# Graph attention and neighbour quantiles on one core: finer pieces of the first search, larger pieces of the quantile sort, the last attention tile in three turns, another order of the units

## The chip, the cores and the metric

One Trainium2 chip, one of its cores. The time is the device time of one execution in microseconds; below, "the profiled execution" is one more execution, taken with the hardware profiler.

## The reference, cut to what matters

There are 4,096 nodes with 128 features and a 0/1 matrix `adj` of 4096 x 4096 with about 32 neighbours in a row. Two layers follow each other.

```python
# layer 0: graph attention, 8 heads
Wh = einsum('nd,hde->hne', x, W)
f1 = einsum('hnd,hd->hn', Wh, a1);  f2 = einsum('hnd,hd->hn', Wh, a2)
e = leaky_relu(f1[:, :, None] + f2[:, None, :], 0.2)
att = softmax(where(adj > 0, e, -9e15), axis=-1)
cat = heads side by side of elu(att @ Wh)
x1 = layernorm(x + elu(cat @ W1 + b1)) * gamma + beta
# layer 1: quantiles over a thinned neighbour list
keep = neighbours whose rank is not a multiple of ceil(number / 2)
agg = mean over q in (0.25, 0.5, 0.75) of the value at place ceil(q * n_keep) - 1
      in each feature's sorted kept neighbours of x1
out = (0.5 * agg + 0.5 * x1) @ Wl.T + bl + x1
```

## The kernel before, in words

Nodes are handled in 32 tiles of 128. The order of instructions on VectorE, TensorE, ScalarE and GpSimd is the order in which the program writes them (`manual_schedule(engines=ORDERED)`); the DMAs of SyncE are placed by the framework. Generators that `yield` are woven into one another by hand, and each yield ends a "piece".

**The first search** (`neighbours`, L624, over the 6 tiles of the first block) turns rows of `adj` into lists of neighbours. Halves of a tile's rows are loaded from ScalarE's DMA queue into three buffers (L635), ScalarE takes their sign (L642), TensorE makes keys from it, 512 columns at a time (two products a piece, L681 and L684), and VectorE finds the largest eight of each 128 (L648) and merges them (L653, L655). There are 8 pieces to a tile. In these pieces `tile_gat_quantile_kernel` (L323 to L326) calls once per piece the generator `node_rows` (L542), which prepares what the gathers read later: it loads W, a1, a2, Wl and x on ScalarE's queue, forms `wa` = W a on VectorE (L565, L568), transposes x tile by tile on TensorE (L585), copies the result on ScalarE (L587), multiplies it by `wa` (L579), copies that (L574), clips it, and stores each node's row with its f2 in `xt_d` (L592). It works on four tiles at a time: in one piece the four transposes and a copy, in the next four products.

**The attention** runs over blocks of 6, 10 and 16 tiles. `fetch_rows` (L909) gathers up to 64 neighbour rows per partition, one indirect DMA of GpSimd a slot, 16 slots to a buffer `G`. `attend` (L935) weighs a tile: add f1 and f2 (L949), leaky relu (L955), exp (L956), per-node sums on TensorE (L964), reciprocal (L974, L975), spreading it back (L980), the product (L991), the block matrix `wide` (L999), and one product a slot into `y` (L1012). It then says "summed", and its tail (from L1024: W, elu, W1, layer norm) is woven into the next tile's head by `step` (L371). The search of the next block is woven in as well. The very last tile has nobody behind it. Its x1 is scattered to `x1_d` (L369), and then the quantiles can start.

**The quantiles**: after all 32 tiles, the tiles are sorted again in 21 units: [0], [1], the pairs [2,3] to [22,23], and [24] to [31]. For a unit, GpSimd gathers its neighbours' x1 slot by slot into one of two buffers `vals` and its own rows into `xs` (L507 to L517). The queue of GpSimd holds, in this order: the gathers of unit i+1, the writes of unit i-1 (L519, which wait for its result on ScalarE), the gathers of unit i+2, and so on; those of a unit wait until the unit two before has read its `vals`. `quantile_out` (L1168) runs a selection network on VectorE: minima and maxima of two runs of slots (L1225), between two work buffers and into `goal`. After a certain time on VectorE, estimated by `then` (L1191), the loop issues `turn_of_gpsimd` (L1194), a copy of one element from PSUM, and starts to count anew. It cuts longer runs:

```python
if then(c * m) > TURN_MAX:            # too long for this turn
    room = int((TURN_AIM - then(0)) / (size * TT_EACH))
...
if ran > TURN_MIN:
    turn_of_gpsimd()
```

Then TensorE takes the weighed sum of the goals (L1244), adds half of x1 (L1251), ScalarE copies it (L1255), TensorE multiplies by Wl (L1258 to L1262), ScalarE copies (L1270), and GpSimd scatters the result to the output.

Of the kernel before, what the change touches and what calls it, by code (L numbers as in the profile page):

```python
# [22 lines left out]
H = 8  # L23
# [219 lines left out]
def kernel(  # L243
# [127 lines left out]
    def step(fetch=None, soon=(), pieces=None, quota=0, first=False, among=()):  # L371
        if first:
            keep_x1(fetch)
        if fetch:
            weigh.append(fetch_rows(tc, attp, fetch, xt_d, list(among)))
        if not first:
            keep_x1(fetch)
        done = 0
        each = quota / STEPS
        head = None  # L380
        if len(weigh) > 1 or (weigh and not fetch):
            head = attend(tc, attp, pp, weigh.pop(0), consts)
# [159 lines left out]
def node_rows(tc, sp, pp, rec, x, W, W_sb, a1, a2, Wl, wa, WlT, ident, bad, xt_d):  # L542
# [28 lines left out]
    xT = f_ps = None  # L571
    for t in range(0, NT + 8, 4):
        if f_ps is not None:
            nc.scalar.copy(F[:, t - 8 : t - 4, :], f_ps)  # L574
            f_ps = None
        if xT is not None:
            f_ps = pp.tile([P, 4, 2 * H], F32, name="f_ps")
            for u in range(4):
                nc.tensor.matmul(f_ps[:, u, :], lhsT=xT[:, ts(u, P)], rhs=wa, start=True, stop=True)  # L579
            xT = None  # L580
        yield
        if t < NT:
            xt_ps = pp.tile([P, 4 * P], F32, name="xt_ps")
            for u in range(4):
                nc.tensor.transpose(xt_ps[:, ts(u, P)], rec[:, t + u, R_X : R_X + D], ident)  # L585
            xT = sp.tile([P, 4 * P], F32, name="xT", bufs=2)
            nc.scalar.copy(xT, xt_ps)  # L587
        yield
# [343 lines left out]
    return R, mine, out  # L932


def attend(tc, ap, pp, fetched, consts):  # L935


    nc = tc.nc
    R, mine, parts = fetched
    own, ownT = consts["own"], consts["ownT"]  # L940
    slots = sum(w - g0 for w, g0, _, _ in parts)


    z = ap.tile([P, L, H], F32, name="z", bufs=2)
    layer = []
    a = 0
    for w, g0, runs, f1v in parts:
        for G, col, g, m in runs:
            nc.vector.tensor_tensor(  # L949
                z[:, a + g : a + g + m, :], G[:, col : col + m, D:], f1v[:, g : g + m, :], ALU.add  # L950
            )
        layer.append(a)
        a += w - g0
    zs = z[:, 0:slots, :].rearrange("p s h -> p (s h)")
    nc.vector.scalar_tensor_tensor(zs, zs, ALPHA, zs, ALU.mult, ALU.max)  # L955
    nc.scalar.activation(zs, zs, AF.Exp)  # L956
    yield

    small = consts["small"]
    den = small[:, 0 : 32 * H]  # L960
    for i, (w, g0, runs, f1v) in enumerate(parts):
        k = P // w
        for r in range(k // 4):
            nc.tensor.matmul(  # L964
                den[0:4, :].rearrange("p (g r h) -> p r g h", r=k // 4, h=H)[:, r, g0:],
                lhsT=own[w][:, ts(r, 4)],
                rhs=z[:, layer[i] : layer[i] + w - g0, :],
                start=(i == 0 and r == 0),
                stop=(i == len(parts) - 1),
                skip_group_check=True,  # L970
            )
    yield
    rden = ap.tile([4, 32 * H], F32, name="rden", bufs=1)
    nc.vector.tensor_scalar(rden, den[0:4, :], TINY, None, ALU.max)  # L974
    nc.vector.reciprocal(rden, rden)  # L975
    rz = pp.tile([P, L * H], F32, name="rz")
    for i, (w, g0, runs, f1v) in enumerate(parts):
        k = P // w
        for r in range(k // 4):
            nc.tensor.matmul(  # L980
                rz[:, layer[i] * H : (layer[i] + w - g0) * H],
                lhsT=ownT[w][:, r, :],
                rhs=rden.rearrange("p (g r h) -> p r g h", r=k // 4, h=H)[:, r, g0:],
                start=(i == 0 and r == 0),
                stop=(r == k // 4 - 1),
                skip_group_check=True,
            )
            if r % 8 == 7:
                yield
    yield  # L990
    nc.vector.tensor_tensor(zs, zs, rz[:, 0 : slots * H], ALU.mult)  # L991

    y = pp.tile([P, 2, 512], F32, name="y")
    yf = y.rearrange("p a b -> p (a b)")
    for i, (w, g0, runs, f1v) in enumerate(parts):
        k, n = P // w, w - g0
        pf = ap.tile([P, H * P], F32, name="wide")
        spread = [P, n, k, H]
        nc.vector.tensor_tensor(  # L999
            pf[:, 0 : n * k * H].rearrange("p (g k h) -> p g k h", g=n, k=k),  # L1000
            z[:, layer[i] : layer[i] + n, :].unsqueeze(2).to_broadcast(spread),
            own[w].unsqueeze(1).unsqueeze(3).to_broadcast(spread),
            ALU.mult,
        )
        yield
        c = k * H
        for G, col, a, m in reversed(runs):

            for j in reversed(range(a, a + m)):
                g = g0 + j  # L1010

                nc.tensor.matmul(  # L1012
                    yf[:, ts(g, c)],
                    lhsT=G[:, col + j - a, 0:D],
                    rhs=pf[:, ts(j, c)],
                    start=(i == 0 and g % (w // 2) == w // 2 - 1),
                    stop=(i == len(parts) - 1),
                    skip_group_check=True,
                )
                if g % 4 == 0:  # L1020
# [4 lines left out]
    nc.scalar.copy(  # L1025
        yT.rearrange("p h (u g) -> p g u h", u=4), yf.rearrange("p (g u h) -> p g u h", u=4, h=H)
    )
# [470 lines left out]
```

## Time and profile before

| | us |
|---|---|
| three runs | 3614.76, 3615.5, 3617.49 |
| median | 3615.5 |
| the profiled execution, its own time | 3611.84 |
| its span, first to last instruction | 3610.1 |
| VectorE busy | 2742.8 (76%), 7,591 instructions |
| GpSimd busy | 2344.3 (65%), 2,341 instructions |
| TensorE busy, its weight loads | 1258.1 (35%) and 951.4 (26%) |
| ScalarE busy | 399.5 (11%) |
| first gather of the attention / of the quantiles | 150.8 / 1828.3 |
| first and last tensor_tensor of the quantiles | 1857.3 / 3596.6 |

In the profile a row of a group gives the line, the engine, the operation, what is written from what, shapes, the count, busy time and mean, then how long the engine was idle before these instructions and who released it. A row of the timeline gives start, duration, engine, line, operation. DVE is VectorE, PE is TensorE and PEld its weight loads, ACT ScalarE, POOL GpSimd, SP SyncE. An fp32 product appears as two TensorE instructions.

### The profile page before, as it was taken

The numbers are of one execution on the slowest core, as the hardware profiler recorded it, in microseconds if no ns is written. First come the engines' busy times: TensorE is split into PE (matmuls) and PEld (weight loads), VectorE is DVE, ScalarE is ACT, GpSimd is POOL, SyncE is SP. The second block draws the span as 40 slices with busy tenths as digits, with TensorE's granted clock in tenths as the row PEclk, the third lists the DMA queues.
The fourth block names the chain that finished last, engine by engine and source line by source line (L and its number), as shares of the span: only waits on it lengthen the run. The fifth ranks groups of instructions, "written<-read, shape, count | busy, mean of one in ns | idle before, by whom it ended". The sixth has DMA issues, their size and how long they took to land. (4 is left out here: it accounts for less than half of the span.)

```text
span 3610.1 us, 22900 instructions
## 1 busy us (share of the span) xinstructions
PE 1258.1 (35%) x5323; PEld 951.4 (26%) x5323; DVE 2742.8 (76%) x7591; ACT 399.5 (11%) x555; POOL 2344.3 (65%) x2341
## 2 busy tenths in 40 slices
PE   6377667878456454456610000000000000001101
PEld 3044545445455454355510000000000000000101
DVE  7787548877345122157448999999999999999998
ACT  3122122322111011111110000000000000000000
POOL 1375767757777777777557776777555766667530
PEclk9965557566556555555555555555555555555555
DMA  6443244432222222222111111111111111111100
GB/s 212 132 147 90 67 149 139 142 123 70 59 63 55 55 55 54 66 58 55 43 38 48 48 47 41 46 47 46 39 34 37 47 44 40 43 45 47 38 20 3
DMA packets 109137, 237.46 MB, mean 66 GB/s; under 512 B 46720, under 2 KB 63104, under 8 KB 100800
## 3 DMA queue, kind: packets, MB, share of 16 engines
q0 software_dynamic: 74368, 156.34, 15.5%
q10 hardware_dynamic: 14848, 70.85, 5.7%
q1 hardware_dynamic: 19776, 8.73, 1.1%
q8 instruction: 44, 0.72, 0.1%
q14 instruction: 101, 0.83, 0.1%
HBM read 224.60 MB, written 11.15 MB: 65 GB/s over the span
## 5 line engine op out<-in xcount | busy, mean ns | idle before, releaser
L219 POOL DMA_INDIRECT G<-xt_d,idx x1124 | 1096.6, 976 | 416.3 <-issue 324.0
L219 POOL DMA_INDIRECT vals<-x_d,idx x1024 | 1052.3, 1028 | 333.9 <-issue 298.0
L1225 DVE TENSOR_TENSOR work<-work 128x512 f32<-128x512 f32 (+6 forms) x1405 | 959.4, 710 | 0.4
L1244 PE MATMUL st_ps<-dg,goal 128*128 128x128 f32 x286 | 71.8, 429 | 1644.7 <-DVE goal L1225 1574.6
L1225 DVE TENSOR_TENSOR work<-work,work 128x512 f32<-128x512 f32 (+5 forms) x958 | 604.9, 655 | 0.7
L1244 PEld LDWEIGHTS st_ps<-dg,goal 128*128 128x128 f32 x286 | 63.8, 324 | 1651.0 <-issue 1650.2
L1012 PE MATMUL y<-wide,G 128*128 128x32 f32 (+3 forms) x2248 | 482.7, 392 | 26.9 <-DVE wide L999 26.9
L1012 PEld LDWEIGHTS y<-wide,G 128*128 128x128 f32 x2248 | 461.2, 309 | 62.3 <-DVE wide L999 30.0
L648 DVE MAX8 first<-key 128x8 f32<-128x128 f32 x1024 | 225.2, 281 | 119.0 <-PE key L684 118.5
L949 DVE TENSOR_TENSOR z<-G,f1x 128x128 f32<-128x128 f32 (+5 forms) x92 | 29.0, 328 | 307.9 <-DMA G<-xt_d,idx 302.7
L228 POOL DMA_INDIRECT out_dram<-o,own_i x32 | 51.0, 1593 | 295.3 <-ACT o L1270 276.1
L681 PE MATMUL key<-sgn,markb 128*128 128x512 bf16 x256 | 149.3, 583 | 145.3 <-DVE first L648 98.2
L1196 DVE COPY junk<-still 128x1 f32<-128x1 f32 x1295 | 191.2, 148 | 0.0
L1225 DVE TENSOR_TENSOR work<-vals 128x1024 f32<-128x1024 f32 (+8 forms) x140 | 138.8, 1007 | 46.2 <-DMA vals<-x_d,idx 45.9
L642 ACT ACTIVATE sgn<-adj_t 128x2048 bf16<-128x2048 int32 x64 | 122.1, 1907 | 355.4 <-PE key L681 304.8
L1043 PE MATMUL small<-W_sb,late 128*128 128x128 f32 x512 | 126.0, 430 | 88.4 <-DVE late L1040 88.4
L1243 ACT ACTIVATE dg<-ident,wt 128x128 f32<-128x128 f32 x143 | 47.5, 393 | 955.9 <-PE st_ps L1244 955.6
L964 PE MATMUL small<-z,own 128*4 128x32 f32 (+6 forms) x438 | 49.6, 280 | 284.8 <-ACT z L956 284.8
L684 PE MATMUL key<-parts,oneb 64*128 64x512 bf16 x256 | 147.2, 575 | 0.2 <-POOL parts L237 0.2
L1043 PEld LDWEIGHTS small<-W_sb,late 128*128 128x128 f32 x512 | 111.7, 324 | 102.7 <-DVE late L1040 99.0
L980 PE MATMUL rz<-rden,ownT 4*128 4x32 f32 (+6 forms) x438 | 97.8, 386 | 78.0 <-DVE rden L975 63.0
L1031 PE MATMUL hT<-late,W_sb 128*128 128x128 f32 x512 | 110.9, 385 | 35.4 <-ACT late L1025 35.4
(184 smaller groups left out, 1763.3 us busy)
## 6 DMA issues: line engine op xcount, KB each, us to landing
adj_t<-in_adj_dram ACTq DMA_DIRECT2D x64, 1024.0 KB
G<-xt_d,idx POOLq DMA_INDIRECT x1124
vals<-x_d,idx POOLq DMA_INDIRECT x1024
R<-rec_d SPq DMA_DIRECT2D x128, 26.2 KB
xt_d<-rec SPq DMA_DIRECT2D x4, 544.0 KB
rec<-in_x_dram ACTq DMA_DIRECT2D x4, 512.0 KB
narrow<-rec_d SPq DMA_DIRECT2D x68, 5.2 KB
a_b<-in_L_gnn_a_dram ACTq DMA_DIRECT2D x2, 512.0 KB
```

The source lines that it names most:

```text
L219: nc.gpsimd.indirect_dma_start(out=dst, out_offset=None, in_=rows, in_offset=bass.IndirectOffsetOnAxis(ap=idx, axis=0),)
L642: nc.scalar.activation(sgn, adj_t, AF.Sign, accum_out=cnt[:, i : i + 1])
L648: nc.vector.max(first[:, ts(c0 // CW + c, 8)], key[:, ts(c, CW)])
L681: nc.tensor.matmul(key, lhsT=markb, rhs=sgn[:, ts(b, 512)], start=True, stop=False)
L684: nc.tensor.matmul(key, lhsT=oneb[0:64, :], rhs=parts[1][:, ts(r - 1, 512)] if r else parts[0], start=False, stop=True)
L980: nc.tensor.matmul(rz[:, layer[i] * H : (layer[i] + w - g0) * H], lhsT=ownT[w][:, r, :], rhs=rden.rearrange("p (g r h) -> p r g h", r=k // ...
L1012: nc.tensor.matmul(yf[:, ts(g, c)], lhsT=G[:, col + j - a, 0:D], rhs=pf[:, ts(j, c)], start=(i == 0 and g % (w // 2) == w // 2 - 1), stop= ...
L1031: nc.tensor.matmul(hT[:, ts(h, P)], lhsT=consts["W_sb"][:, h, :], rhs=yT[:, h, :], start=True, stop=True)
L1043: nc.tensor.matmul(o, lhsT=hv[:, h, :], rhs=consts["W1_sb"][:, h, :], start=(h == 0), stop=(h == H - 1))
L1196: nc.vector.tensor_copy(junk, late["still"])
L1225: nc.vector.tensor_tensor(slots_of(dst, (j, c, s, m), size), slots_of(a, (i, c, s, m), size), slots_of(b, (i + d, c, s, m), size), op,)
L1244: nc.tensor.matmul(st_ps[:, u, :], lhsT=goal[:, (j * k + u) * D : (j * k + u + 1) * D], rhs=dg, start=(j == 0), stop=False,)
```

## The change

Four parts in one edit.

```diff
-TURN_MIN, TURN_AIM, TURN_MAX = 1.25, 1.45, 1.7
+TURN_MIN, TURN_AIM, TURN_MAX = 1.1, 1.9, 2.4
```

The quantile loop cuts fewer runs of slots. By its own counting, with the constants before, it issues 2,649 tensor_tensors and 1,295 copies; with those after, 2,250 and 1,118, on the same elements.

```diff
-    order = UNITS[:1] + UNITS[2 + len(pairs) :] + pairs[::-1] + UNITS[1:2]
+    order = UNITS[:2] + UNITS[2 + len(pairs) :] + pairs[::-1]
```

Unit [1] is sorted second and not last; the pair [2,3] is now the last.

```diff
@@ node_rows
     load = nc.scalar.dma_start
+    for _ in range(4):
+        yield
     load(W_sb, W.rearrange("h d e -> d h e"))
-    yield
+    for _ in range(2):
+        yield
...
     for i in range(4):
-        for _ in range(3):
+        for _ in range(2):
             yield
...
+    LAG = 3
+    turned, f_ps = [], None
+    for t in range(NT + LAG):
+        if t < NT:
+            xt_ps = pp.tile([P, 4 * P], F32, name="xt_ps")[:, 0:P]
+            nc.tensor.transpose(xt_ps, rec[:, t, R_X : R_X + D], ident)
+            xT = sp.tile([P, P], F32, name="xT", bufs=LAG + 2)
+            nc.scalar.copy(xT, xt_ps)
+            turned.append(xT)
+        u = t - LAG
+        if u >= 0:
+            if u % 4 == 0:
+                f_ps = pp.tile([P, 4, 2 * H], F32, name="f_ps")
+            nc.tensor.matmul(f_ps[:, u % 4, :], lhsT=turned.pop(0), rhs=wa, start=True, stop=True)
+        yield
+        if u > 0 and u % 4 == 3:
+            nc.scalar.copy(F[:, u - 3 : u + 1, :], f_ps)
```

In the first search, one transpose with its copy and one product go into each piece; the product belongs to the tile three pieces back. W is loaded four pieces later, a1, a2 and Wl five. These rows now take 55 pieces where they took 39, of the search's 62.

```diff
@@ attend
+    turns = [(parts, 0)]
+    if last and [v[0:2] for v in parts] == [(32, 0)]:
+        w, g0, runs, f1v = parts[0]
+        turns = []
+        for m, (a, b) in enumerate(((0, 16), (16, 24), (24, 32))):
+            G, col, g, _ = runs[a // 16]
+            turns.append(([(w, a, [[G, col + a - g, 0, b - a]], f1v[:, a:b, :])], a))
...
+    for turn, (parts, a0) in enumerate(turns):
...
```

The body of `attend`, from the addition to the products into `y`, stands in this loop. For all tiles but the very last it runs once and issues what it issued before. For the last tile it runs over slots 0 to 15, 16 to 23 and 24 to 31 in turn, each with its own exp, sums, reciprocal, `wide` and products; `step` passes `last` when no fetch and no other tile follows.

More of the change, by code (lines that the diff above doesn't have):

```diff
@@ L381, in step @@
         if len(weigh) > 1 or (weigh and not fetch):
-            head = attend(tc, attp, pp, weigh.pop(0), consts)
+            last = not fetch and len(weigh) == 1
+            head = attend(tc, attp, pp, weigh.pop(0), consts, last)
         active = [v for v in (tail.pop() if tail else None, head) if v]
@@ L570, in node_rows @@
     F = sp.tile([P, NT, 2 * H], F32, name="F")
[L571 to L580, printed above, removed]
-        yield
[L582 to L588, printed above, removed]
+    LAG = 3
[12 more added lines that the diff above has]
+            nc.tensor.matmul(f_ps[:, u % 4, :], lhsT=turned.pop(0), rhs=wa, start=True, stop=True)
+        yield
+        if u > 0 and u % 4 == 3:
+            nc.scalar.copy(F[:, u - 3 : u + 1, :], f_ps)
     for dst, src in ((R_F1, F[:, :, 0:H]), (R_X + D, F[:, :, H:])):
@@ L932, in fetch_rows, with attend @@
     return R, mine, out
-def attend(tc, ap, pp, fetched, consts):
+def attend(tc, ap, pp, fetched, consts, last):
     nc = tc.nc
@@ L940, in attend @@
     own, ownT = consts["own"], consts["ownT"]
-    slots = sum(w - g0 for w, g0, _, _ in parts)
-    z = ap.tile([P, L, H], F32, name="z", bufs=2)
[L945 to L954, printed above, removed]
@@ L955, in attend @@
-    nc.vector.scalar_tensor_tensor(zs, zs, ALPHA, zs, ALU.mult, ALU.max)
-    nc.scalar.activation(zs, zs, AF.Exp)
-    yield
+    turns = [(parts, 0)]
[5 more added lines that the diff above has]
+            turns.append(([(w, a, [[G, col + a - g, 0, b - a]], f1v[:, a:b, :])], a))
+    z = ap.tile([P, L, H], F32, name="z", bufs=2)
@@ L959, in attend @@
     small = consts["small"]
     den = small[:, 0 : 32 * H]
[L961 to L971, printed above, removed]
@@ L972, in attend @@
-    yield
     rden = ap.tile([4, 32 * H], F32, name="rden", bufs=1)
-    nc.vector.tensor_scalar(rden, den[0:4, :], TINY, None, ALU.max)
-    nc.vector.reciprocal(rden, rden)
     rz = pp.tile([P, L * H], F32, name="rz")
[L977 to L989, printed above, removed]
@@ L990, in attend @@
-    yield
-    nc.vector.tensor_tensor(zs, zs, rz[:, 0 : slots * H], ALU.mult)
     y = pp.tile([P, 2, 512], F32, name="y")
     yf = y.rearrange("p a b -> p (a b)")
[L995 to L1004, printed above, removed]
+    opened = set()
@@ new lines, in attend @@
+    for turn, (parts, a0) in enumerate(turns):
+        whole = len(turns) == 1
+        layer = []
+        a = a0
+        for w, g0, runs, f1v in parts:
+            for G, col, g, m in runs:
+                nc.vector.tensor_tensor(
+                    z[:, a + g : a + g + m, :],
+                    G[:, col : col + m, D:],
+                    f1v[:, g : g + m, :],
+                    ALU.add,
+                )
+            layer.append(a)
+            a += runs[-1][2] + runs[-1][3]
+        zs = z[:, a0:a, :].rearrange("p s h -> p (s h)")
+        nc.vector.scalar_tensor_tensor(zs, zs, ALPHA, zs, ALU.mult, ALU.max)
+        nc.scalar.activation(zs, zs, AF.Exp)
@@ L1005, in attend @@
         yield
[L1006 to L1010, printed above, removed]
+        for i, (w, g0, runs, f1v) in enumerate(parts):
+            k = P // w
+            g1 = g0 + runs[-1][2] + runs[-1][3]
+            for r in range(k // 4):
                 nc.tensor.matmul(
[L1013 to L1016, printed above, removed]
+                    den[0:4, :].rearrange("p (g r h) -> p r g h", r=k // 4, h=H)[:, r, g0:g1],
+                    lhsT=own[w][:, ts(r, 4)],
+                    rhs=z[:, layer[i] : layer[i] + g1 - g0, :],
+                    start=(turn == 0 and i == 0 and r == 0),
@@ L1019, in attend @@
                 )
-                if g % 4 == 0:
-                    yield
+        yield
+        rd = rden if whole else rden[:, a0 * H : a * H]
+        nc.vector.tensor_scalar(
+            rd, den[0:4, :] if whole else den[0:4, a0 * H : a * H], TINY, None, ALU.max
+        )
+        nc.vector.reciprocal(rd, rd)
+        for i, (w, g0, runs, f1v) in enumerate(parts):
+            k = P // w
+            n = runs[-1][2] + runs[-1][3]
+            for r in range(k // 4):
+                nc.tensor.matmul(
+                    rz[:, layer[i] * H : (layer[i] + n) * H],
+                    lhsT=ownT[w][:, r, :],
+                    rhs=rden.rearrange("p (g r h) -> p r g h", r=k // 4, h=H)[:, r, g0 : g0 + n],
+                    start=(turn == 0 and i == 0 and r == 0),
+                    stop=(r == k // 4 - 1),
+                    skip_group_check=True,
+                )
+                if r % 8 == 7:
+                    yield
+        yield
+        nc.vector.tensor_tensor(zs, zs, rz[:, a0 * H : a * H], ALU.mult)
+        for i, (w, g0, runs, f1v) in enumerate(parts):
+            k, n = P // w, runs[-1][2] + runs[-1][3]
+            pf = ap.tile([P, H * P], F32, name="wide")
+            spread = [P, n, k, H]
+            nc.vector.tensor_tensor(
+                pf[:, 0 : n * k * H].rearrange("p (g k h) -> p g k h", g=n, k=k),
+                z[:, layer[i] : layer[i] + n, :].unsqueeze(2).to_broadcast(spread),
+                own[w].unsqueeze(1).unsqueeze(3).to_broadcast(spread),
+                ALU.mult,
+            )
+            yield
+            c = k * H
+            for G, col, a, m in reversed(runs):
+                for j in reversed(range(a, a + m)):
+                    g = g0 + j
+                    bank = g * c // 512
+                    nc.tensor.matmul(
+                        yf[:, ts(g, c)],
+                        lhsT=G[:, col + j - a, 0:D],
+                        rhs=pf[:, ts(j, c)],
+                        start=bank not in opened,
+                        stop=(i == len(parts) - 1),
+                        skip_group_check=True,
+                    )
+                    opened.add(bank)
+                    if g % 4 == 0:
+                        yield
     yield "summed"
```

## Prediction

> **What bounds the kernel now.** I read the busy shares and the 40 slices first. Each slice is 90 us.
>
> ```profile
> DVE  7787548877345122157448999999999999999998
> ...
> POOL 1375767757777777777557776777555766667530
> ```
>
> Three stages follow one another. The first search fills slices 1 and 2. After it GpSimd's gathers set the pace up to about slice 20. From slice 23 VectorE is at nine tenths or more, to the end. The busy times by stretch say the same: 896.7 of 1,630 us for VectorE between 150 and 1780 us, but 1,723.9 of 1,740 between 1857 and 3597. So a microsecond saved in the quantile stage on VectorE, or before the first gather, or between the last gather of the rows and the first one of the quantiles, comes off the end one for one.
>
> Next, VectorE's groups with the shapes kept apart, for what the quantile stage is made of (count, busy us, mean ns):
>
> ```profile
> L1225 DVE TENSOR_TENSOR work<-work 128x512 f32<-128x512 f32 x512 | 339.3, 682 | 0.1
> L1225 DVE TENSOR_TENSOR work<-work 128x1024 f32<-128x1024 f32 x273 | 334.2, 1229 | 0.0
> ...
> L1196 DVE COPY junk<-still 128x1 f32<-128x1 f32 x1295 | 191.2, 148 | 0.0
> ...
> L1225 DVE TENSOR_TENSOR work<-vals 128x512 f32<-128x512 f32 x21 | 13.8, 686 | 13.8 <-DMA vals<-x_d,idx 13.8
> ```
>
> These busy times overlap, so prices must be taken from start to start, in the timeline:
>
> ```profile
> 2311.64 0.68 DVE L1225 TENSOR_TENSOR work<-work 128x512 f32<-128x512 f32 x1
> 2312.17 0.97 POOL L219 DMA_INDIRECT vals<-x_d,idx  x1 [0.30 <-issue]
> 2312.23 0.42 DVE L1225 TENSOR_TENSOR work<-work,work 128x256 f32<-128x256 f32 x1
> 2312.57 0.42 DVE L1225 TENSOR_TENSOR work<-work 128x256 f32<-128x256 f32 x1
> 2312.90 0.15 DVE L1196 COPY junk<-still 128x1 f32<-128x1 f32 x1
> 2312.97 1.62 DVE L1225 TENSOR_TENSOR work<-work 128x256 f32<-128x256 f32 x3
> 2313.44 1.23 POOL L219 DMA_INDIRECT vals<-x_d,idx  x1 [0.30 <-issue]
> ```
>
> A 512 takes 0.59 to 0.61 us to the next start, a 256 0.34, a copy 0.07. Hence 1.054 ns an element, 0.067 us fixed for a tensor_tensor, 0.070 for a copy. Counting through the loop of quantile_out gives 1,382,784 elements, and the rows have 2,649 tensor_tensors: 1457.5 + 177.5 + 90.7 (1,295 copies) = 1725.7 us. Measured: 3596.6 - 1857.3 - 13.8 waiting = 1725.5. The prices hold.
>
> **Quantile pieces.** The same loop with 1.1/1.9/2.4 issues 2,250 tensor_tensors and 1,118 copies on the same elements. Saved: 399 x 0.067 = 26.7 and 177 x 0.070 = 12.4, together **39.1 us**, all on VectorE's path. The Trainium skill (Perfetto Trace Analysis, Optimizing Scalar/DVE Operations) puts a VectorE instruction's overhead at about 60 ns on SBUF and 125 ns on PSUM, and the copy reads PSUM; that would make 23.9 + 22.1 = 46.0. The copies here cost 0.070 from start to start, so I take 39.1. Bounds 33 (some overheads reappear as semaphore waits) to 46.
>
> What hides behind VectorE are the gathers: 0.94 us each and 0.30 of issue, a cycle of 1.25. A gather that is delayed ends 0.90 us after a boundary between two VectorE instructions: the one above starts at 2313.44, the next copy is at 2314.51, and it lasts 1.23 rather than 0.94. Of 1,038 gathers between 1860 and 3462 us, 930 go through beside a copy and 108 between two tensor_tensors. Here a rule speaks against the change: by the skill (SBUF — State Buffer, Who interferes with whom) a VectorE instruction with two SBUF inputs keeps out, for its whole length, a GpSimd instruction that reads SBUF. Pieces of up to 2048 elements (2.2 us) then hold a gather that much longer. I count with one gather a turn, and no gather cycle under 1.25 us. Turns now average 1.32 us, after the change 1.50.
>
> Is that enough? The pairs [18,19] down to [4,5] have 559 turns now and 434 after. While they are sorted, GpSimd must fetch the seven pairs [14,15] to [2,3] (402 gathers) and write 16 tiles: 418. So 16 turns are spare, some 25 us. Followed gather by gather (one per turn, vals free after its last read), the lead of a pair's last gather over its first tensor_tensor comes out within 7 us of the trace for today's kernel (140 against 139 at [18,19], 87 against 87 at [4,5]). After the change it falls from 115-123 us at [18,19] to 22 at [2,3], and VectorE never waits in the pairs. By the rule without spare turns it would wait; by this count, no cost.
>
> **Two short units first.** VectorE waits twice at the start: 22 gathers, then 13.8 us for [24] (the row above). With [1] second, its 22 gathers fit beside the sort of [0] (35 us). But [24] then needs 22 + 1 + 36 gathers from 1857, at some 1.33 each 79 us, plus 1.65 to land, against 67 us of sorting: the wait only moves, to 14-17 us. I take **+2** (bounds -3 to +4). The end gets longer: the last unit is now a pair. Today:
>
> ```profile
> 3600.96 0.27 ACT L1270 COPY o<-fo_ps 128x128 f32<-128x128 f32 x1 [2.04 <-PE fo_ps L1262]
> 3601.50 0.96 POOL L228 DMA_INDIRECT out_dram<-o,own_i  x1 [24.39 <-ACT o L1270]
> ```
>
> From the last goal (3596.6) to the end of that copy are 4.6 us. For [2,3] it was 7.7 (3564.4 to 3572.06), and its second write waited 1.56 us for the first to land:
>
> ```profile
> 3572.33 2.26 POOL L228 DMA_INDIRECT out_dram<-o,own_i  x1 [59.48 <-ACT o L1270]
> 3576.15 0.96 POOL L228 DMA_INDIRECT out_dram<-o,own_i  x1 [1.56 <-DMA out_dram<-o,own_i]
> ```
>
> With an idle VectorE the first takes 0.96, so the second starts 2.5 later: 3.1 + 2.5 = **+5.6** (3 to 8).
>
> **First search.** The busy times by stretch of 5 us (PE, PE loads, VectorE, ...):
>
> ```profile
> 20.00:25.00 5.00, 1.49 (x3) 0.20 (x2) 0.33 (x2) 2.64 (x3) 0.00 (x0) 1.00 0.93 315
> ...
> 50.00:55.00 5.00, 5.00 (x17) 2.86 (x16) 3.43 (x17) 0.91 (x3) 0.00 (x0) 1.00 0.36 149
> ```
>
> From 45 to 80 us TensorE is full and VectorE idle for 8.7 us. Two pieces there take TensorE 4.79 us from start to start: four key products at 0.54, four transposes 0.91, four products 1.72. VectorE's two take 3.3. Spread out, a piece costs TensorE 1.08 + 0.23 + 0.43 = 1.74 against 1.66: idle 0.08 x 32 = 2.6 and some semaphores. ScalarE's 32 small copies (0.27 each, 8.6 us for 8 x 0.58) lie beside this; it is busy 12.8 of these 35 us. Gain **5.5** (2 to 8). The second piece: the third sign activation starts at 21.46, straight after four DMA issues (W, two of a, Wl; 17.18 to 21.41) that stand ahead of it on ScalarE's queue, and VectorE starves from 19.9 to 24.7. Those issues now stand behind it. But the products of W and a, at piece 16 as before, are reached earlier and may wait for a. The four loads of x move from pieces 6, 9, 12 and 15 to 10, 12, 14 and 16; the first transpose is at piece 18 as before, 13 us behind its load. Gain **3** (-2 to 4.8). The rows are stored some 15 pieces later, near 100 us on SP's queue, whose next work is at 144; their first reader is the gather at 150.8. Covered; without cover it would cost the overshoot.
>
> **Last tile.** Its second half holds VectorE's and ScalarE's queues, and with them the tail of the tile before:
>
> ```profile
> 1768.13 0.37 DVE L949 TENSOR_TENSOR z<-G,f1x 128x128 f32<-128x128 f32 x1
> ...
> 1781.39 0.38 DVE L949 TENSOR_TENSOR z<-G,f1x 128x128 f32<-128x128 f32 x1 [12.89 <-DMA G<-xt_d,idx]
> ...
> 1808.38 1.87 ACT L1025 COPY late<-y 128x1024 f32<-128x1024 f32 x1 [9.42 <-PE y L1012]
> ```
>
> With turns, the first 16 slots wait only for ScalarE's copy (to 1774.2) and a table load (1.28): weights 1775.8, sums and reciprocal 1778.0, spread 1780.5, the tail's two VectorE steps 1782.4. Then TensorE runs 8 products of W1 (3.8) and 16 slots (0.43 each, from 56 instructions in 12.07): 1793.0. Each further turn is a chain of sums (0.6), reciprocal (0.75), rz (0.5), two VectorE steps (0.65) and semaphores (0.3), with TensorE idle, then 8 slots (3.45): 1799.3 and 1805.5, against 1808.3. Gain **3** (0 to 6), although all rows had landed at 1781: TensorE is the limit.
>
> **Sum.** 39.1 - 2 - 5.6 + 5.5 + 3 + 3 = 43.0. The profiled execution took 3611.84 us (span 3610.1); 43 less is 3568.8. The median of the runs stands 3.7 higher: **3572 us**.
>
> **Rivals.**
> - *The gathers fall out of step* (the slower side). If a waiting gather misses its turn more often than the 16 spare turns allow, VectorE waits at the start of the pairs, 1.25 us for each missing gather. It eats the whole 43 us from 34 + 16 = 50 misses in 418 on, one in eight. At one in five: 84 - 16 = 68 gathers, 85 us: 3657. For it: 2.2 us pieces are not in this trace (its longest tensor_tensor lasts 1.6). Against it: none of the 930 copy boundaries went by with a gather waiting, and gathers held for 0.4 us went in at the next. 4%.
> - *A milder form*, one in ten: 42 - 16 = 26 gathers, 32 us, less some of the lead: about 3595, still faster. 7%.
> - *The two front parts give nothing*: the search bound by its loads (315 GB/s in slice 1), the last tile by TensorE. 3572 + 11.5 = 3583.5. For it: the loads are near full up to 45 us. Against it: from 45 to 80 they are at a quarter. 15%.
> - *More than counted*: a copy close to 125 ns and no delay of VectorE by gathers: 3562. 6%.
> - That the last tile is not split: it is 32 slots in two G tiles, as the two 128x128 additions show, which is what the new test asks. Inside the third.
>
> The likeliest, 3572, has 67%, its own range 3564 to 3581; 1% is left for no difference. About 0.2% (7 us) is what a measurement of this kernel tells from none. Faster 95%, within 1%, slower 4%. The range 3559 to 3590 takes in the third and fourth case and leaves the starving ones out.
>
> **What would show it.** The rows of line 1225 must sum to 2,250 and the copies to 1,118, and the quantile stage on VectorE, waits left out, to 1686 us. One wait of about 15 us before the second or third unit; any wait for vals later is the first rival. The first gather of G near 142 instead of 150.8; no slice of VectorE near 0.33 of 5 us at 20. From the last piece to the end 19 us instead of 13.5. The forecast falls if gathers last much longer than the turn they wait for.

## The result, and the profile after

The changed kernel takes 3561.55 us (median of 4 runs, 3556.80 to 3566.22); the kernel before took 3615.13 (4 runs, 3607.50 to 3617.49). The ratio is 0.9855, with a 95% interval of 0.9834 to 0.9876. 3572 was predicted. Five of the runs below (copies in the pairs, two turns, the changed kernel again, the first of all three together, small pieces in the single units) fell in executions in which every kernel, the one before too, took 700 to 1,000 us longer, with waits that the trace calls remote, and of these only what happens inside a stage is read.

The profiled execution took 3564.49 us, its span 3562.7: 47.4 less than before. Cut into stages, with the prediction's terms beside them:

| stage, us | before | after | change | predicted |
|---|---|---|---|---|
| start to the first gather of G | 150.8 | 138.1 | -12.7 | -8.5 |
| first to last gather of G | 1627.9 | 1630.2 | +2.3 | 0 |
| last gather of G to the first of vals | 49.6 | 45.5 | -4.1 | -3 |
| from there to the first tensor_tensor of the quantiles | 29.0 | 29.0 | 0 | 0 |
| quantile stage on VectorE, waits left out | 1725.5 | 1683.8 | -41.7 | -39.1 |
| waits in it | 13.8 | 17.4 | +3.6 | +2 |
| last piece to the end of the span | 13.5 | 18.6 | +5.2 | +5.6 |
| sum | 3610.1 | 3562.7 | -47.4 | -43.0 |

First the busy shares in 40 slices, as before:

```profile
DVE  8787458877435222257548999999999999999997
...
POOL 1475767657777777777757777788777677787870
```

The picture is the old one: VectorE is still at nine tenths or more from slice 23 to the last but one. GpSimd, which had slackened to 5 and 6 near the end, is now at 7 and 8 to the last but one slice, with one 6: a gather counts as busy while VectorE holds it, and the gathers' lead is smaller. Next the shapes of the quantile stage (count, busy us, mean ns | idle before):

```profile
L1251 DVE TENSOR_TENSOR work<-work 128x512 f32<-128x512 f32 x367 | 245.3, 686 | 0.2
...
L1251 DVE TENSOR_TENSOR work<-work 128x1024 f32<-128x1024 f32 x179 | 218.5, 1224 | 0.1
...
L1222 DVE COPY junk<-still 128x1 f32<-128x1 f32 x1118 | 169.0, 151 | 0.0
...
L1251 DVE TENSOR_TENSOR work<-work 128x2048 f32<-128x2048 f32 x45 | 102.6, 2285 | 0.0
```

In the groups of this form, 512 elements come 367 times instead of 512, 1024 come 179 times instead of 273, and 2048 are new. All groups together are 2,250 tensor_tensors and 1,118 copies, the numbers counted ahead. The tile vals shows all that VectorE waited for (us, times):

```profile
  DMA vals<-x_d,idx: 49.6, 2
```

32.2 of it is the first arrival, which lies before the stage; 17.4 is the one wait for [24]. No pair waited. In the first search, two stretches of 5 us (PE, PE loads, VectorE, ScalarE, ...):

```profile
20.00:25.00 5.00, 3.84 (x8) 0.76 (x8) 4.35 (x19) 1.65 (x1) 0.00 (x0) 1.00 0.94 333
...
50.00:55.00 5.00, 5.00 (x18) 2.38 (x18) 4.90 (x22) 1.66 (x6) 0.00 (x0) 1.00 0.63 206
```

VectorE is busy for 4.35 us where it was busy for 0.33, and for 4.90 where it had 3.43. The last tile on TensorE (start, us):

```profile
1775.93 5.17 PE L1037 MATMUL y<-wide,G 128*128 128x32 f32 x24
...
1783.81 3.62 PE L1037 MATMUL y<-wide,G 128*128 128x32 f32 x16 [0.84 <-DVE wide L1021]
...
1790.15 3.62 PE L1037 MATMUL y<-wide,G 128*128 128x32 f32 x16 [0.84 <-DVE wide L1021]
...
1795.79 3.78 PE L1057 MATMUL hT<-late,W_sb 128*128 128x128 f32 x16 [2.01 <-ACT late L1051]
```

The products into `y` of the first turn end at 1781.1, the other turns run 1783.8 to 1787.4 and 1790.2 to 1793.8. So TensorE pauses 2.7 us from one turn to the next, and a turn takes 3.62: the chain was put at 2.8 + 3.45. At the end:

```profile
3551.01 0.37 ACT L1296 COPY o<-fo_ps 128x256 f32<-128x256 f32 x1 [2.27 <-PE fo_ps L1288]
3551.66 0.96 POOL L228 DMA_INDIRECT out_dram<-o,own_i  x1 [58.23 <-ACT o L1296]
3554.14 0.96 POOL L228 DMA_INDIRECT out_dram<-o,own_i  x1 [1.53 <-DMA out_dram<-o,own_i]
```

The last piece ends at 3544.1, so the copy's end (3551.4) is 7.3 us behind it, where 7.7 was read from [2,3] before, and the second write is 2.48 behind the first, where 2.5 was put.

### The profile page after: what moved, and what is told of

The parts are those of the page before. It is cut to its first block, busy times and chain, and to the rows that moved or that the text cites. A ratio compares the mean times of both kernels' runs of the same rounds, so it can differ in the third digit from the quotient of the medians.

```text
span 3562.7 us, 22331 instructions
## 1 busy us (share of the span) xinstructions
PE 1261.9 (35%) x5331; PEld 952.1 (27%) x5331; DVE 2701.3 (76%) x7026; ACT 403.6 (11%) x581; POOL 2507.5 (70%) x2341
## 5 line engine op out<-in xcount | busy, mean ns | idle before, releaser
L219 POOL DMA_INDIRECT vals<-x_d,idx x1024 | 1214.5, 1186 | 315.7 <-issue 306.9
L1251 DVE TENSOR_TENSOR work<-work 128x512 f32<-128x512 f32 (+7 forms) x1194 | 933.7, 812 | 0.6
L1251 DVE TENSOR_TENSOR work<-work,work 128x512 f32<-128x512 f32 (+6 forms) x821 | 590.7, 741 | 0.5
L1037 PE MATMUL y<-wide,G 128*128 128x32 f32 (+3 forms) x2248 | 492.2, 398 | 25.0 <-DVE wide L1021 24.9
L1037 PEld LDWEIGHTS y<-wide,G 128*128 128x128 f32 x2248 | 469.8, 314 | 61.9 <-DVE wide L1021 28.0
L1251 DVE TENSOR_TENSOR work<-vals 128x1536 f32<-128x1536 f32 (+7 forms) x96 | 133.3, 1404 | 50.0 <-DMA vals<-x_d,idx 49.6
L1222 DVE COPY junk<-still 128x1 f32<-128x1 f32 x1118 | 169.0, 151 | 0.0
L228 POOL DMA_INDIRECT out_dram<-o,own_i x32 | 46.4, 1449 | 116.6 <-ACT o L1296 94.4
```

Source lines behind the costliest of these rows:

```text
L219: nc.gpsimd.indirect_dma_start(out=dst, out_offset=None, in_=rows, in_offset=bass.IndirectOffsetOnAxis(ap=idx, axis=0),)
L1037: nc.tensor.matmul(yf[:, ts(g, c)], lhsT=G[:, col + j - a, 0:D], rhs=pf[:, ts(j, c)], start=bank not in opened, stop=(i == len(parts) - 1) ...
L1222: nc.vector.tensor_copy(junk, late["still"])
L1251: nc.vector.tensor_tensor(slots_of(dst, (j, c, s, m), size), slots_of(a, (i, c, s, m), size), slots_of(b, (i + d, c, s, m), size), op,)
```

## The experiments

The theory was the prediction's: the terms add up, copies and tensor_tensors cost a fixed amount each, and gathers hide as long as they get one boundary per turn. Its rivals were that the gathers fall out of step, and that the two front parts give nothing. Stages of each profile, in us (the quantile stage without waits is "sort"):

| | span | first gather | G stretch | to vals | sort | waits | tail |
|---|---|---|---|---|---|---|---|
| before | 3610.1 | 150.8 | 1627.9 | 49.6 | 1725.5 | 13.8 | 13.5 |
| after | 3562.7 | 138.1 | 1630.2 | 45.5 | 1683.8 | 17.4 | 18.6 |
| small pieces | 3598.7 | 137.8 | 1628.6 | 46.4 | 1725.1 | 12.8 | 19.0 |
| short unit last | 3553.4 | 137.7 | 1628.1 | 46.3 | 1683.8 | 15.6 | 13.0 |
| four at once | 3568.6 | 147.0 | 1626.6 | 46.2 | 1683.7 | 17.4 | 18.7 |
| last tile whole | 3558.5 | 137.9 | 1622.9 | 49.4 | 1683.9 | 17.4 | 18.2 |
| no copies | 3590.4 | 138.2 | 1632.0 | 47.4 | 1645.6 | 79.3 | 18.9 |
| fewer turns | 3674.6 | 138.1 | 1634.8 | 46.4 | 1667.1 | 140.8 | 18.6 |
| all three again | 3544.9 | 138.1 | 1626.3 | 44.2 | 1655.9 | 38.4 | 13.1 |

**Small pieces.** The new kernel with the old cuts.

```diff
-TURN_MIN, TURN_AIM, TURN_MAX = 1.1, 1.9, 2.4
+TURN_MIN, TURN_AIM, TURN_MAX = 1.25, 1.45, 1.7
```

> The changed kernel with the turn constants of before (1.25, 1.45, 1.7), all else as changed. If the price per instruction is the cause (0.067 us a tensor_tensor, 0.070 a copy, 399 and 177 of them), the quantile stage on VectorE without its wait goes back from 1683.9 to 1725 us, and the span grows by some 41 us to about 3604; the lead of the last gather over the first tensor_tensor at [2,3] goes back from 14 to about 85 us. If instead the larger pieces saved by something other than instruction count (fewer delays by the gathers), the stage comes back by clearly less or more than the 39 us that the counts give; the stretch of the wait before [24] tells whether the 3.6 us more there belong to the pieces (then back to about 14) or to the order (then 17).

Measured: 3600.43 us (one run; before 3612.68 there). Its VectorE groups by shape are again those of before:

```profile
L1251 DVE TENSOR_TENSOR work<-work 128x512 f32<-128x512 f32 x512 | 341.8, 690 | 0.1
...
L1222 DVE COPY junk<-still 128x1 f32<-128x1 f32 x1295 | 199.3, 154 | 0.0
```

The sort returns to 1725.1, and nothing else in the table moves by more than the runs do, but for a wait that is 4.6 shorter. The pieces are worth 41.3 us here, against 41.7 from before to after: they carry the change. The lead at [2,3] is back at 84.7 us (14.1 in the changed kernel).

**Short unit last.** [1] sorted last again.

```diff
-    order = UNITS[:2] + UNITS[2 + len(pairs) :] + pairs[::-1]
+    order = UNITS[:1] + UNITS[2 + len(pairs) :] + pairs[::-1] + UNITS[1:2]
```

> The changed kernel with [1] sorted last again, all else as changed. My theory: the order costs, so this is faster than the changed kernel by 5 us at the end (13.5 us from the last piece to the end of the span instead of 18.6) and by 0 to 3 us in the wait before [24] (14 to 15 instead of 17.4): span about 3555. The rival, that two short units first save a wait: slower, span 3565 to 3580, with a second wait behind [0] or [24].

Measured: 3554.84 us median of 4 (3547.41 to 3557.15), ratio 0.9837 (0.9818 to 0.9856). The last write in its timeline (GpSimd) shows what the order costs:

```profile
3544.86 0.96 POOL L228 DMA_INDIRECT out_dram<-o,own_i  x1 [25.01 <-ACT o L1296]
```

It is the only one behind the last piece (3540.4), and the tail is 13.0 us again. The wait for [24] stays, at 15.6 before it. With small pieces it was 13.8 in the old order and 12.8 in the new, with large ones 15.6 and 17.4: so the pieces lengthen it by 1.8 to 4.6, and the order by -1.0 to +1.8. The new order thus removes no wait and costs 5.6 us at the end.

**Four at once.** The loads stay late, but a piece has no work of its own: four transposes, then four products, as before.

```diff
-    for t in range(NT + LAG):
+    for t in range(0, NT + 8, 4):
...
...
+            for u in range(4):
+                nc.tensor.matmul(f_ps[:, u, :], lhsT=xT[:, ts(u, P)], rhs=wa, start=True, stop=True)
...
+            for u in range(4):
+                nc.tensor.transpose(xt_ps[:, ts(u, P)], rec[:, t + u, R_X : R_X + D], ident)
```

> The changed kernel with the loads of W, a, Wl and x in their new places, but four transposes and then four products a piece, as before. It splits the 12.7 us by which the first gather came earlier. My theory: the gap of VectorE at 20 us stays closed (4 us of the 12.7), and TensorE's full pieces come back from 45 to 80 us with 7 to 9 us of idle VectorE: first gather at 145 to 148 instead of 138.1. Rival, the loads explain nearly all of it: first gather at 138 to 141. Rival, the pieces explain all: 150.

Measured: 3570.35 us (one run). The same two stretches as above, of this kernel:

```profile
20.00:25.00 5.00, 3.98 (x8) 0.72 (x7) 4.53 (x21) 2.00 (x2) 0.00 (x0) 1.00 0.99 367
...
50.00:55.00 5.00, 5.00 (x18) 2.88 (x17) 3.50 (x14) 2.49 (x3) 0.00 (x0) 1.00 0.02 3
```

The hole at 20 us is filled here too (4.53): that was the order of the loads. The one at 50 us is back (3.50): that was the four at once. The first gather comes at 147.0. So spreading is worth 8.8 us and the loads 3.9, where 5.5 and 3 were put.

**Last tile whole.**

```diff
-            last = not fetch and len(weigh) == 1
+            last = False
```

> The changed kernel with the last tile weighed at once, all else as changed. My theory: the distance from the last gather of the rows to the first of the quantiles, 45.6 us in the changed kernel and 49.6 before, goes back to 49 to 50; span about 3567. Rival, that these 4 us came from the earlier stages (a buffer of G free earlier): it stays at 45 to 46.

Measured: 3560.22 us (one run). GpSimd at the end of the rows (start, us; the gathers of vals begin 49.4 after the first of these lines):

```profile
1760.73 0.94 POOL L219 DMA_INDIRECT G<-xt_d,idx  x1 [0.30 <-issue]
...
1782.59 0.96 POOL L228 DMA_INDIRECT x_d<-x_t,mine  x1 [13.57 <-DVE x_t L1109]
```

In the changed kernel the distance is 45.5 (1768.32 to 1813.85). Six profiles with the last tile in three turns have 45.5 to 47.4 there, the two with it whole 49.4 and 49.6: the three turns give 2.0 to 4.1 us at their place. That this run's whole span is shorter than the changed kernel's all the same (by 4.2) lies in the stretch of the gathers of G, which is 7.3 shorter here and differs by up to 11.9 (1622.9 to 1634.8) between executions that do the same work there.

**No copies.** What a waiting gather needs was the basis of the count of gathers, and of the rival. Small cuts, and no copy at all:

```diff
-        nc.vector.tensor_copy(junk, late["still"])
+        pass
-TURN_MIN, TURN_AIM, TURN_MAX = 1.1, 1.9, 2.4
+TURN_MIN, TURN_AIM, TURN_MAX = 1.25, 1.45, 1.7
```

> The changed kernel without the one-element copies, with runs cut as before (1.25, 1.45, 1.7): 2,649 tensor_tensors, no copy. It asks whether a waiting gather needs the copy or goes in between any two VectorE instructions. If any boundary will do (108 of 119 boundaries between two tensor_tensors in the trace of before let one in), VectorE's stage is 1725 - 91 = 1635 us plus waits of about 14 before [24] and 26 in the last three pairs, span about 3540, and gathers stay near 1.3 us a cycle. If only a copy lets one in, hardly a gather passes while VectorE sorts and each unit waits for nearly all of its own at 1.25 us each: some 1,300 us more, span above 4500.

Measured: 3592.22 us (one run). It fits neither reading: much shorter than if a gather needed a copy, longer than if it got into every boundary. VectorE's waits for vals, from the tile's own view (us, times):

```profile
  DMA vals<-x_d,idx: 110.6, 8
```

Less the first arrival, that is 79 us of waiting. The sort fell to 1645.6 (1635.0 by count: 1457.5 + 177.5). At the boundaries of two tensor_tensors a gather or write that VectorE held went in 957 times; 108 such boundaries passed with one waiting. In the kernel before it is 935 taken beside a copy, 109 taken and 12 passed between tensor_tensors, in the changed one 1,014 taken and 2 passed beside a copy, 31 and 34 between tensor_tensors. (These counts shift by a few with how close to a boundary an end must lie.) One entry accounts for the longest of the waits, 24.6 us at [6,7] (GpSimd's timeline of this kernel):

```profile
3208.82 1.08 POOL L228 DMA_INDIRECT out_dram<-o,own_i  x1 [0.30 <-issue]
3211.44 49.89 POOL L228 DMA_INDIRECT out_dram<-o,own_i  x1 [1.53 <-DMA out_dram<-o,own_i]
3261.63 0.98 POOL L219 DMA_INDIRECT vals<-x_d,idx  x1 [0.30 <-issue]
```

The second write of a pair took 49.9 us, where they took 1 to 3 in the kernel before and in the changed one. Beside it VectorE ran one tensor_tensor after another, from 3212.5 on of 1024 or 512 elements, with no copy among them. Its timeline shows the last of them:

```profile
3247.70 9.30 DVE L1251 TENSOR_TENSOR work<-work 128x1024 f32<-128x1024 f32 x10
3256.91 6.04 DVE L1251 TENSOR_TENSOR work<-work,work 128x1024 f32<-128x1024 f32 x7
3262.88 0.68 DVE L1251 TENSOR_TENSOR work<-work 128x512 f32<-128x512 f32 x1
```

48 boundaries passed until it went through. Nearly all the passes of this run fall on five entries, held for 2.9, 4.1, 12.7, 13.5 and 49.9 us. Each of the five went in at the first boundary at which VectorE paused, for 34 or 35 ns, which it does at 82 of its 2,648 boundaries here, and all 38 held entries that met a pause of 30 ns or more went in at it. The pauses stand at the same instructions (47 of 47) in the profiles of the changed kernel, of four at once and of the last tile whole, so the program places them, not the gathers. Without copies nearly all gathers get in at once, but one that is passed over can stay out until VectorE next pauses. Whether a pause put there on purpose would do as well as a copy wasn't tried.

**Fewer turns.** Copies kept, but pieces of at least 1.5 and at most 3.2 us.

```diff
-TURN_MIN, TURN_AIM, TURN_MAX = 1.1, 1.9, 2.4
+TURN_MIN, TURN_AIM, TURN_MAX = 1.5, 2.5, 3.2
```

> The changed kernel with 1.5/2.5/3.2: by count 2,239 tensor_tensors and 835 copies, fewer copies than the 1,088 entries on GpSimd's queue. If any boundary lets a gather in, VectorE waits some 22 us in the last three pairs and the span is about 3570. If a gather needs a copy, the gathers fall behind in every unit from [25] on: waits of over 250 us, span about 3825.

Measured: 3676.50 us (one run), slower than before and between the two forecasts. The sort is 1667.1 us (1666.0 by count), but VectorE's waits for vals, in the same view, are:

```profile
  DMA vals<-x_d,idx: 157.4, 11
```

Less the first arrival, VectorE waits some 125 us for vals. With two waits that the trace lays to nothing it is 140.8 us: 21.4 before [24], 12.6 to 25.6 at each pair from [14,15] to [4,5], and 6.6 at [2,3]. Boundaries between tensor_tensors took 284 gathers and let 147 pass, copies took all of their 643. A gather cycle beside the sort is now 1.42 to 1.81 us. This is the slower rival, in a kernel that has too few turns: its mechanism exists, and the changed kernel stops short of it.

**Copies in the pairs.** In the changed kernel the gathers' lead grows over the single units, from 14 us at [25] to 99 at [20,21]; do they need all their copies? On top of the short unit last, copies are left only in [0] and in the pairs before the last:

```diff
-        nc.vector.tensor_copy(junk, late["still"])
+        if unit[0] == 0 or k == 2 and unit[0] > 2:
+            nc.vector.tensor_copy(junk, late["still"])
```

> [1] last again, and the copies issued only in [0] and the pairs [4,5] to [22,23]; the other units have the same pieces and no copy. 503 of the 1,118 copies fall away, 35 us at 0.070. Without copies a gather's cycle in the single units was 1.34 to 1.43 us, and each single unit has 65 us and more for 37 to 43 gathers, so I expect no new wait: VectorE's stage without waits 1649 to 1655, span about 3519. Rival: a gather needs the copies in the single units too, or one is locked out for tens of microseconds: then waits before the pairs or inside them of 20 us and more, span above 3540.

**Two turns.** On top of the changed kernel:

```diff
-        for m, (a, b) in enumerate(((0, 16), (16, 24), (24, 32))):
+        for m, (a, b) in enumerate(((0, 16), (16, 32))):
```

> The changed kernel with the last tile in two turns, slots 0 to 15 and 16 to 31. My chain says that a turn costs TensorE about 2.8 us of waiting, and that all rows have landed before the second turn begins: the distance from the last gather of the rows to the first of the quantiles goes from 45.5 to about 43 us. Rival, that smaller turns hide more: it goes to 46 or more.

**The changed kernel again**, on the same chip, with no edit.

> The changed kernel itself, on the same chip as the other two, for the comparison: span 3555 to 3565, the stage on VectorE without waits within 1 us of 1683.8, and 17.4 us of wait before [24]; whatever differs from the first profile by more shows how far a single profile can be trusted, the attention's stretch above all (1622.9 to 1630.2 us so far).

Measured, for these three: 4246.97, 4297.82 and 4304.61 us, and 4547.99 for the kernel before. Inside the stages, with waits of over 0.3 us left out, the sort is 1690.1 us for the changed kernel and 1658.7 without 503 of its copies, that is 0.062 us a copy. From the last gather of G to the first of vals it is 90.2 us with two turns (90.6 in the two later runs of this kind), against 92.5 and 91.0 with three: up to two us, of the sign expected, but no more than these distances vary by. Whether the missing copies bring waits can't be read here: no pair waited in these profiles, whose gathers' lead the disturbance had raised.

**All three together**: short unit last, copies in the pairs, two turns. The edits are those three. It ran twice, on two chips.

> The changed kernel with three edits that the runs point to: [1] last, copies only in [0] and the pairs [4,5] to [22,23], and the last tile in two turns of 16. The run of the middle edit fell on a chip where every kernel took some 730 us longer, the one before too, so its span says nothing; this repeats it. My theory: 5 us at the end and 2 before [24] for the order, 31 to 35 us for 503 copies, 2 to 3 us for the turns: span about 3519, ratio to the kernel before about 0.974. Rivals: gathers locked out in the single units without copies (waits of 20 us and more before or inside the pairs, span above 3540); two turns no better than three (the distance from the last gather of the rows to the first of the quantiles 45.5 us or more).

Measured: 4285.10 us against 4583.91 before; the sort is 1659.2, the tail 13.4.

> The same kernel as the last one, again, since that run too fell where the kernel before took 4,584 us. What holds there should hold here: VectorE's stage without waits near 1659 minus what the disturbance added to the changed kernel's (6 us), so 1653; 13.2 us from the last piece to the end; 2 to 3 us less than 45.5 from the last gather of the rows to the first of the quantiles. Span about 3519 and ratio to the kernel before about 0.974, if no new wait opens before or inside the pairs; above 3540 if one does.

The second time it took 3550.51 us (median of 4, 3546.72 to 3551.04), ratio 0.9836 (0.9820 to 0.9853), which doesn't set it apart from the short unit last alone (0.9837). The rival of the expectation came true: the span is 3544.9, not 3519. Against the changed kernel the sort fell by 27.9 to 1655.9, but the waits for vals, in the same view, are:

```profile
  DMA vals<-x_d,idx: 68.8, 4
```

That is two more waits, 13.7 us inside [6,7] and 7.4 inside [4,5]. Beside the single units a gather cycle is now 1.47 to 1.60 us (units [25] to [30]; 1.35 to 1.46 in the changed kernel), and three gathers were kept out there for 3.6, 4.7 and 10.2 us, so the lead at [18,19] is 57.6 instead of 115.1, and it is used up by [8,9]. Of 28 us, 21 became waiting at the other end of the stage.

**Small pieces in the single units**, without copies there, to make more boundaries for the gathers:

```diff
+    least, aim, most = (1.25, 1.45, 1.7) if k == 1 else (TURN_MIN, TURN_AIM, TURN_MAX)
...
-                    if then(c * m) > TURN_MAX:
+                    if then(c * m) > most:
...
-                    if ran > TURN_MIN:
+                    if ran > least:
```

> The last kernel, with the single units cut as before the change (1.25, 1.45, 1.7), still without copies there. In the last kernel the gathers' cycle beside the single units was 1.47 to 1.60 us, the lead at [18,19] 58 us instead of 115, and VectorE waited 21 us at [6,7] and [4,5]. Without copies but with small pieces the cycle was 1.34 to 1.43. If the length of a piece is what slows them, 170 more tensor_tensors cost 11 us (stage without waits about 1667), the lead at [18,19] is back near 100 us and the late waits shrink to under 6: span about 3537. If the missing copies are, the cycle stays at 1.5 and the waits too: span about 3555.

Measured: 4369.52 us against 4601.32. The cycle of units [26] to [30] is 1.33 to 1.36 us, where the first run of all three had 1.40 to 1.56: shorter pieces do shorten it. The lead at [18,19] is 99, but it was 100 in that run too, so it tells nothing. The sort is 1673.2, 14.0 above it. And beside [31] one gather was kept out for 85.7 us (GpSimd's timeline, then the busy times of that stretch in the order used above):

```profile
3205.53 85.74 POOL L219 DMA_INDIRECT vals<-x_d,idx  x1 [11.57 <-DVE work L1253]
...
3205.50:3291.00 85.50, 0.00 (x0) 0.00 (x0) 85.47 (x146) 0.00 (x0) 85.47 (x1) 0.50 0.00 0
```

VectorE ran 146 tensor_tensors in that time, back to back, until its next pause of 35 ns. Small pieces thus don't stop a gather from being kept out; the lead went from 166 us at [22,23] to 82 at [20,21]. Whether the waits of 21 us would vanish, which would leave some 7 us as a gain, isn't measured and stays open.

## Why the prediction was right, and where its terms were off

It forecast faster, at 3572 in a range of 3559 to 3590, and 3561.55 is inside, though 2.5 below the 3564 to 3581 that it gave its likeliest case. Of the 11 us between (3572.5 before rounding), 4.4 are in the sum (47.4 instead of 43.0). The other 6.6 come from where the profiled executions lie among the runs: the one of before was 3.7 below its median, and the sum was carried over with that; the one of after is 2.9 above its own; that is chance. The terms' own errors cancel in part: the gain was put 8.3 us too low in four stages and 3.9 too high in two.

- **Quantile pieces** (39.1): right in mechanism and count; 41.7 by the trace, 41.3 by undoing it. The 2.6 too little lie in the delay of VectorE beside gathers, whose change the sum left out. From start to start over the whole stage, the tensor_tensors during which a gather or write goes in took 7.3 us more than the price before and 1.9 after; the other tensor_tensors took 7.9 and 6.3 less, the copies 0.4 and 1.7 more. Together that is 0.1 us under the price before and 2.7 after. The larger prices, which would have made 46.0 (60 and 125 ns by the Trainium skill, Perfetto Trace Analysis, Optimizing Scalar/DVE Operations), are excluded: a copy takes 0.070 us from start to start before and 0.072 after, and taking copies out gave 0.055 to 0.062 us each in three pairs of runs (503 copies for 27.9 and 31.4 us, 1,295 for 79.5). The case "more than counted" gave the nearest number, 3562, by a cause that the runs deny.
- **Gathers** (no cost): no pair waited, as said. But the lead at [2,3] fell to 14.1 us, not 22, some eight gathers from a wait (1.65 us to land, then 1.5 each), and the run with pieces a third longer went past it. The rule that a VectorE instruction with two inputs in SBUF (the Trainium skill, SBUF — State Buffer, Who interferes with whom) holds a GpSimd read for its length fits the gathers that end 0.90 us after a boundary; what it costs depends on whether a gather gets in at the next boundary, which the rule leaves open: at a copy it did in 1,014 of 1,016 cases, between tensor_tensors it could be passed over 48 times in a row. What spoke against the rival, that no copy had been passed, held but for two.
- **Two short units first** (+2 and +5.6): +3.6 and +5.2. "The wait only moves" held; it came out at 17.4 us because a gather took 1.42 us there from start to start, not 1.33; undoing the order gave 5.6 + 1.8 us back.
- **First search** (5.5 and 3): 8.8 and 3.9. The term mis-sized is a piece of TensorE's. It was put at 1.74 us against VectorE's 1.66, leaving an idle 2.6 us. TensorE's timeline of the changed kernel, one piece and the start of the next:

```profile
75.74 0.59 PE L685 MATMUL key<-sgn,markb 128*128 128x512 bf16 x1
76.26 0.60 PE L688 MATMUL key<-parts,oneb 64*128 64x512 bf16 x1
76.79 0.48 PE L581 MATMUL xt_ps<-ident,rec 128*128 128x128 f32 x1
77.06 0.45 PE L589 MATMUL f_ps<-wa,xT 128*128 128x16 f32 x2
77.35 0.59 PE L685 MATMUL key<-sgn,markb 128*128 128x512 bf16 x1
```

From key product to key product are 1.61 us: 0.52 + 0.53 for the keys, 0.27 for the transpose (put at 0.23) and 0.29 for the product (put at 0.43). That is less than VectorE's 1.66, so nearly all of VectorE's idle time went: from 45 to 80 us it is busy for 33.75 us of 35, before for 26.31, which is 7.4 of the 8.8. The feared wait for a did not come: between 25 and 45 us VectorE is busy for 4.86 to 4.93 of each 5, as before. (The 315 GB/s that the third rival names for slice 1 belong to the stretch from 20 to 25 us; slice 1 of the page has 212.)
- **Last tile** (3): 4.1 between these two profiles, 2.0 to 4.1 over all of them. The chain per turn, 2.8 + 3.45, measured 2.7 + 3.62; the first turn was quicker than put: its products ended 12.8 us behind the last gather of G (1781.1 - 1768.3), where 14.3 were put (1793.0 - 1778.7). That the two front parts give nothing is refuted by both runs.
- Not predicted: the stretch of the gathers of G, +2.3. It lies between 1622.9 and 1634.8 over the profiles with the same work there; why it varies stays open. An instance, GpSimd's wait for TensorE before the same gather (the 385th of G), in the kernel before:

```profile
706.77 1.03 POOL L219 DMA_INDIRECT G<-xt_d,idx  x1 [3.03 <-PE y L1012]
```

and in the changed one:

```profile
696.16 1.04 POOL L219 DMA_INDIRECT G<-xt_d,idx  x1 [8.03 <-PE y L1037]
```

## What to carry to other kernels

Price small instructions from start to start in the stage that bounds the kernel, count them in the loop, and the saving of fewer and larger ones comes out within a few per cent. Count as well what such instructions let through on another engine: past a certain length the saving turns into waits at the far end of the stage, as the runs with longer pieces and with fewer copies show. An average rate hides this: what matters is the one gather that is kept out, and smaller pieces alone didn't prevent it. An order that is meant to remove a wait at the start of a stage has to be priced at the end of it too; here the wait moved, and the end cost 5 us.

## What the runs showed of the hardware beyond that

A gather that waits for VectorE ends 0.90 us after a boundary between two VectorE instructions. At a one-element copy it practically always got in (1,014 of 1,016; in the run with small pieces one gather missed two copies and was held for 4.1 us). Between two tensor_tensors it got in at 957 boundaries of 1,065 without copies, 284 of 431 with long pieces and 31 of 65 in the changed kernel. The passes are not spread evenly: without copies they fall on a few entries, held for up to 49.9 us over 48 boundaries; with small pieces in the single units and no copies there, one was held for 85.7 us over 144. In these traces no boundary at which VectorE paused for 30 ns or more let a held entry pass; all that were passed between tensor_tensors were back to back. Why some back-to-back boundaries let one in and others don't isn't settled.

Without copies the tensor_tensors took 10.6 us more than by count (1645.6 against 1635.0). Those beside which a gather goes in took 15.2 us more than the price, against 6.4 with copies and the same pieces (small pieces): that part of a copy's cost is one that the gathers cause anyway.
